# A convolution, attention and mixture kernel: another order for the first three images of its first part, and VectorE as a second engine for their norms and copies

## The chip, the cores and the metric

The kernel runs on one core of a Trainium2 chip. The metric is the device time of one execution in microseconds (us), given as the median over several executions. The engines are TensorE (PE in the profile), VectorE (DVE), ScalarE (ACT), GpSimd (POOL) and SyncE (SP, which issues the transfers). "PEld" is TensorE's weight load.

## The reference

The input is x with 32 images of 128 channels and 64x64 pixels. Layer 0 normalises each image over groups of four channels, multiplies it from both sides with complex 64x64 matrices (products of butterfly factors), mixes the channels at each of the 64x64 frequencies with weights that went through such matrices too, transforms back and adds the result to x. Layer 1 is an attention over channels and a mixture of eight experts on the 4096 tokens of each image. Only the beginning of layer 0 matters here:

```python
def _gn(v, G=32, eps=1e-5):
    g = v.reshape(B_, G, C_ // G, H_, W_)
    m = jnp.mean(g, axis=(2, 3, 4), keepdims=True)
    s = jnp.var(g, axis=(2, 3, 4), keepdims=True)
    return ((g - m) / jnp.sqrt(s + eps)).reshape(v.shape)

x_f = tensor_product(xc, _c(k11), _c(k12), False)      # both axes of every image
prod = jnp.einsum('bihw,oihw->bohw', x_f, w_f)         # channels mixed at each frequency
out = tensor_product(prod, _c(k21), _c(k22), True)
x = x + jnp.real(out)
```

## The kernel before

The kernel has three parts. The first takes the 32 images one by one through the forward transform and writes `xf` to memory. The second mixes the channels, the third transforms back and does layer 1. The change is in the first part alone.

An image goes through these stages in the first part. All of it is in fp32.

- Load: eight transfers of 256 KB (`load`, L325), issued by SP, into one of three buffers `x`.
- Norm: eight `bn_stats` (`stats`, L332) and one aggregation on VectorE; a tiny matmul that averages over the group (`means`, L345); three tiny steps on VectorE (L350 to L352); a second tiny matmul (`variances`, L355); one tiny step (L358); a power on GpSimd (`power`, L362, for images 0 to 3 also a product and a sign, L365 and L366); then x is scaled in four quarters of 128x1024 (`scaled`): on ScalarE for images 0 to 3 (L373), on VectorE for all others (L375).
- `pz`: four groups of eight 128x128 transposes (`turn_over`, L386). Each group's result in PSUM is copied to `z` in four pieces of 64x512, two for each half r (`turned`, L396, all on ScalarE).
- `pv`: eight groups of 32 small matmuls along one axis (`along_w`, L409), each of which needs the whole of `z`. Each result is copied to `v` as 128x1024 (`w_out`, L420, all on ScalarE).
- `pf`: eight groups of eight matmuls along the other axis (`along_h`, L431), each of which needs the whole of `v`. Each result is copied to `f` (`h_out`, L441: ScalarE for two of eight groups, VectorE for the others) and stored to `xf` by two transfers (`store`, L449).

TensorE needs two instructions in the profile for each fp32 matmul, but one for a transpose. PSUM gives this part four buffers of two banks, used by `pz`, `pv`, `pf` and the tiny matmuls alike.

The order of all instructions is written out before the kernel runs. `add` enters each step with an engine, an estimated length, a due time `at` (in slots of 27.5) and what it comes after; `Plan.run` then plays these lists through and gives each engine, whenever it is free, the ready step with the earliest due time. On TensorE alone the order is the one in which the steps were entered. The finished lists are executed in order by each engine: what stands behind a waiting instruction waits too.

In steady state a slot `s` holds `pz` of image s, `pv` of image s-1 and `pf` of image s-2, interleaved in four quarters. At the start the same loop is used, so slot 0 has `pz` of image 0 alone, slot 1 `pz` of image 1 and `pv` of image 0, and slot 2 the first slot with all three stages. The matrices `pw` and `ph` of these stages are made on VectorE at the very beginning by six butterfly levels (`level`, L234 to L240; then `input_matrices`, L246 to L249).

Of the kernel before, what the change touches and what calls it, by code (L numbers as in the profile page):

```python
# [103 lines left out]
def kernel(  # L104
# [15 lines left out]
    nc = tc.nc  # L120
    B = x.shape[0]
# [11 lines left out]
    pf = dram.tile([n, n, P * n], F32, name="pf")  # L133
# [42 lines left out]
    with ExitStack() as ph1:  # L176
# [12 lines left out]
        def add(key, engine, us, at, run, after=(), take=(), free=(), late=0.0):  # L189
            after = [made[k] for k in after if k in made]  # L190
            if engine == "PE":
                after += on_pe[-1:]
            made[key] = plan.add(engine, us, SLOT * at, run, after, take, free, late)
            if engine == "PE":
                on_pe.append(made[key])
# [132 lines left out]
        def stats(b, k):  # L328
# [3 lines left out]
                nc.vector.bn_stats(tile_of["bs", b][:, k, :], xs[b][:, k * 512 : (k + 1) * 512])  # L332
            return run

        def group_norm(b):

            v = {}

            def moments():
                v["mv"] = st.tile([P, 2], F32, name=f"gmv{b}", tag="gmv", bufs=2)  # L340
                nc.vector.bn_aggr(v["mv"], tile_of["bs", b].rearrange("p k s -> p (k s)"))

            def means():
                v["ps"] = pp.tile([P, 2, 512], F32, tag="ps", name=f"gps{b}")
                nc.tensor.matmul(v["ps"][:, 0, 0:1], gmean, v["mv"][:, 0:1], start=True, stop=True)  # L345

            def spread():
                ms, mv = st.tile([P, 4], F32, name=f"gms{b}", tag="gms", bufs=2), v["mv"]
                v["ms"] = ms
                nc.vector.tensor_copy(ms[:, 0:1], v["ps"][:, 0, 0:1])  # L350
                nc.vector.tensor_sub(ms[:, 1:2], mv[:, 0:1], ms[:, 0:1])
                nc.vector.scalar_tensor_tensor(ms[:, 2:3], ms[:, 1:2], ms[:, 1:2], mv[:, 1:2], ALU.mult, ALU.add)  # L352

            def variances():
                nc.tensor.matmul(v["ps"][:, 0, 1:2], gmean, v["ms"][:, 2:3], start=True, stop=True)  # L355

            def shifted():
                nc.vector.tensor_scalar_add(v["ms"][:, 3:4], v["ps"][:, 0, 1:2], GN_EPS)  # L358

            def power():  # L360
                v["rstd"] = st.tile([P, 1], F32, name=f"grstd{b}", tag="grstd", bufs=2)
                nc.gpsimd.tensor_tensor(v["rstd"], v["ms"][:, 3:4], mhalf[:, 0:1], ALU.pow)  # L362
                if b < 4:
                    v["nmr"] = st.tile([P, 1], F32, name=f"gnmr{b}", tag="gnmr", bufs=2)
                    nc.gpsimd.tensor_tensor(v["nmr"], v["ms"][:, 0:1], v["rstd"], ALU.mult)  # L365
                    nc.gpsimd.tensor_scalar_mul(v["nmr"], v["nmr"], -1.0)  # L366

            def scaled(k):
                def run():
                    part = xs[b][:, k * 1024 : (k + 1) * 1024]  # L370
                    if b < 4:

                        nc.scalar.activation(part, part, AF.Identity, bias=v["nmr"], scale=v["rstd"])  # L373
                        return
                    nc.vector.tensor_scalar(part, part, v["ms"][:, 0:1], v["rstd"], ALU.subtract, ALU.mult)  # L375
                return run

            return moments, means, spread, variances, shifted, power, [scaled(k) for k in range(4)]

        def turn_over(b, g):  # L380
# [5 lines left out]
                    nc.tensor.transpose(pv[:, k, :], xs[b][:, h * n : (h + 2) * n], ident)  # L386
            return run

        def turned(b, g, r):

            def run():
                if g == 0 and r == 0:
                    zs[b] = zp.tile([P, n, n], F32, tag="z", name=f"z{b}")
                pv = tile_of["pz", b, g].rearrange("w u (k c) -> w (u k) c", c=P)
                for half in range(2):
                    nc.scalar.copy(  # L396
                        zs[b][half * n : (half + 1) * n, :, 32 * r + 8 * g : 32 * r + 8 * g + 8],
                        pv[r * n : (r + 1) * n, :, half * n : (half + 1) * n].rearrange("w h c -> w c h"),
                    )
            return run  # L400
# [14 lines left out]
        def w_out(b, g):  # L415

            def run():
                if g == 0:
                    vs[b] = vp.tile([P, n, P], F32, tag="v", name=f"v{b}")
                nc.scalar.copy(  # L420
                    vs[b].rearrange("h w (a c) -> h w a c", a=2)[:, :, :, 8 * g : 8 * g + 8],
                    tile_of.pop(("pv", b, g)).rearrange("h a (c w) -> h w a c", w=n),
                )
            return run
# [45 lines left out]
        def piece_of_image(b, k):  # L470

            add(
                ("x", b, k), "SP", 0.45, b - 2 + 0.1 * k, load(b, k),
                [("pz", b - 3, g) for g in range(4)] + [("x", b, k - 1), ("pf", b - 4, k)],
                ("x",) if k == 0 else (), (), 4.0,
            )

        def norm(b):

            at = b - 1  # L480
            for k in range(8) if b < 4 else ():
                piece_of_image(b, k)
            for k in range(8):
                add(("bn", b, k), "DVE", 0.7, at + 0.01 * k, stats(b, k), [("x", b, k), ("nm", b - 2, 3), ("bn", b, k - 1)])

        def norm_on_pe(b, step):
            if not 0 <= b < B:
                return
            at = b - 0.9
            if step == 0:  # L490
                gn = tile_of["gn", b] = group_norm(b)
                add(("ag", b), "DVE", 0.4, at, gn[0], [("bn", b, k) for k in range(8)])
                add(("g1", b), "PE", 0.3, at, gn[1], [("ag", b)], ("ps",))
                add(("gm", b), "DVE", 0.7, at, gn[2], [("g1", b)])
            else:
                gn = tile_of.pop(("gn", b))
                add(("g2", b), "PE", 0.3, at, gn[3], [("gm", b)])
                add(("gr", b), "DVE", 0.25, at, gn[4], [("g2", b)], (), ("ps",))
                add(("gp", b), "POOL", 0.6 if b >= 4 else 1.6, at, gn[5], [("gr", b)])
                for k in range(4):  # L500
                    add(("nm", b, k), *(("DVE", 0.85) if b >= 4 else ("ACT", 1.05)), at + 0.01 * k, gn[6][k], [("gp", b)])

        def piece(kind, b, g, at):
            if not 0 <= b < B:
                return
            if kind == "pz":
                add(
                    ("pz", b, g), "PE", 1.0, at, turn_over(b, g), [("nm", b, k) for k in range(4)],
                    ("ps",), ("x",) if g == 3 else (),
                )  # L510
                for r in range(2):
                    add(
                        ("zo", b, g, r), "ACT", 1.2, at, turned(b, g, r),
                        [("pz", b, g)] + [("pv", b - 2, k) for k in range(8)] + ([("zo", b, 0, 0)] if g or r else []),
                        (), ("ps",) if r else (),
                    )
            elif kind == "pv":
                add(
                    ("pv", b, g), "PE", 1.12, at, along_w(b, g),
                    [("zo", b, k, r) for k in range(4) for r in range(2)] + ["wi"], ("ps",),  # L520
                )
                add(
                    ("vo", b, g), "ACT", 1.02, at, w_out(b, g),
                    [("pv", b, g)] + [("pf", b - 2, k) for k in range(8)] + ([("vo", b, 0)] if g else []), (), ("ps",),
                )
            else:
                add(("pf", b, g), "PE", 1.95, at, along_h(b, g), [("vo", b, k) for k in range(8)], ("ps",))
                on_act = g % 4 == 3
                add(("fo", b, g), "ACT" if on_act else "DVE", 1.02 if on_act else 1.22, at, h_out(b, g), [("pf", b, g)], ("f",), ("ps",))
                add(("fs", b, g), "SP", 0.9, at, store(b, g), [("fo", b, g)], (), ("f",), 5.0)  # L530
# [4 lines left out]
        norm(1)  # L535
        norm_on_pe(0, 0)
        norm_on_pe(0, 1)
        for s in range(B + 2):
            if s == 0:
                norm(2)  # L540
            for g in range(4):
                at = s + 0.25 * g
                if g == min(s, 3) - 1:
# [6 lines left out]
                for k in range(2):  # L550
                    piece("pf", s - 2, 2 * g + k, at + 0.12 + 0.07 * k)
                    if 4 <= s + 2 < B:
                        piece_of_image(s + 2, 2 * g + k)
            if 3 <= s + 2 < B:
                norm(s + 2)
            if s == 0:
                norm_on_pe(1, 0)
                norm_on_pe(1, 1)
            if s == 3:
                butterfly(0, "POOL", nc.gpsimd, 3.2, 4.5)  # L560
                add("sel", "POOL", 2.5, 99, select, [("nm", 4, 3)])
# [8 lines left out]
            if 12 <= s < 16:  # L570
                k = s - 12
# [11 lines left out]
    with ExitStack() as ph2:  # L583
# [162 lines left out]
        for w in range(n):  # L746
# [9 lines left out]
            for half in range(2):  # L756
                for t in range(4):
                    at = w + 0.5 * half + 0.125 * t
# [784 lines left out]
```

## Time and profile before

| | us |
|---|---|
| median of 4 runs | 5922.15 (5916.55 to 5925.2) |
| the profiled execution | 5922.91, of which 5921.1 are its span |
| TensorE busy | 5787.2 (98%) |
| VectorE busy | 4234.0 (72%) |
| ScalarE busy | 3830.1 (65%) |
| GpSimd busy | 3944.3 (67%) |
| TensorE's first transpose (image 0) | 21.12 |
| first `pv` of image 0 | 39.06 |
| first transpose of image 3 | 87.68 |
| last `pf` of the first part ends | about 928 |

The span runs from the first to the last instruction. All times within it are counted from its start. The page of the profile gives busy times and a strip of 40 slices of the span for each engine, in tenths; the timeline lists instructions in order with the idle time before them and what ended it.

### The profile page before, as it was taken

How to read it: one execution, taken by the hardware profiler on the slowest of the kernel's cores; microseconds unless marked ns; L12 is line 12 of the kernel's file. 1: busy time of each engine (PE TensorE's matmuls, PEld its weight loads, DVE VectorE, ACT ScalarE, POOL GpSimd, SP SyncE). 2: the span in 40 equal slices, each digit the busy share in tenths (PEclk: the TensorE clock that was granted, in tenths of full speed). 3: DMA queues.
4: the chain of work that ended last, by engine and by line, in shares of the span. 5: the costliest groups of instructions: out<-in, count | busy, mean ns of one | idle time of the engine just before them, and what ended most of it. 6: DMA issues, size and time to landing. Idle time of an engine off the chain costs nothing.

```text
span 5921.1 us, 221064 instructions
## 1 busy us (share of the span) xinstructions
PE 5787.2 (98%) x94348; PEld 4559.5 (77%) x94348; DVE 4234.0 (72%) x10353; ACT 3830.1 (65%) x7089; POOL 3944.3 (67%) x4210
## 2 busy tenths in 40 slices
PE   7999999999999999989999999999999999999997
PEld 7999999999999999976666666666666666666653
DVE  5565555555555555537888878788888888787877
ACT  7666664555555555457777777777777777777762
POOL 2110006666666666607888888888888888888887
PEclk9999999999999999989999999999999999999999
DMA  5766667666666666652322222222223222222201
GB/s 196 239 228 234 236 212 208 172 170 173 172 172 172 172 172 173 162 153 61 97 76 87 78 79 87 82 88 83 89 75 97 76 84 81 79 86 84 77 21 29
DMA packets 664682, 756.90 MB, mean 128 GB/s; under 512 B 70608, under 2 KB 462288, under 8 KB 659600
## 3 DMA queue, kind: packets, MB, share of 16 engines
q1 hardware_dynamic: 661088, 733.69, 42.4%
q8 instruction: 741, 12.14, 0.9%
q0 software_dynamic: 2608, 9.06, 0.5%
q14 instruction: 245, 2.01, 0.1%
HBM read 406.79 MB, written 335.54 MB: 125 GB/s over the span
## 4 chain that ended last, share of the span: by engine, by line
PE 81%; DVE 12%; ACT 3%; issue 2%; POOL 2%; DMA 1%; SPq 0%; DVEq 0%; POOLq 0%; ACTq 0%
PE pe L1323 24%; PE m L671 17%; PE g L649 10%; PE pf L431 7%; PE pu L910 4%; PE py L933 4%; PE pp L1185 4%; PE pg L1112 4%; DVE tm L1334 4%; PE pv L409 3%; DVE bs L1035 2%; PE pz L386 1%; ACT z L396 1%; PE px L1310 1%; PE pt L1066 1%
## 5 line engine op out<-in xcount | busy, mean ns | idle before, releaser
L1323 PE MATMUL pe<-ew_sb,xT 128*128 128x512 f32 x4096 | 1973.3, 600 | 36.4 <-DVE tm L1334 22.6
L1334 DVE TENSOR_TENSOR tm<-pe,oh 128x512 f32<-128x512 f32 x2028 | 1296.0, 676 | 369.7 <-PE pe L1323 261.6
L1359 POOL TENSOR_TENSOR tm<-tm 128x512 f32<-128x512 f32 x1014 | 1269.3, 1270 | 291.0 <-DVE tm L1334 287.1
L1323 PEld LDWEIGHTS pe<-ew_sb,xT 128*128 128x128 f32 x4096 | 692.0, 190 | 551.6 <-issue 325.5
L660 DVE COPY f<-g 128x1024 f32<-128x1024 f32 x508 | 622.0, 1224 | 649.7 <-PE g L649 649.6
L671 PE MATMUL m<-f,s 128*64 128x64 f32 x32768 | 1070.6, 224 | 2.4 <-issue 1.6
L671 PEld LDWEIGHTS m<-f,s 128*64 128x64 f32 x32768 | 1000.6, 138 | 63.7 <-issue 3.0
L617 POOL COPY s<-l 128x512 f32<-128x512 f32 x512 | 547.3, 1105 | 524.1 <-issue 507.9
L660 ACT COPY f<-g 128x1024 f32<-128x1024 f32 x508 | 514.4, 1013 | 561.8 <-PE g L649 535.3
L1362 POOL TENSOR_TENSOR tk<-tk,tm 128x256 f32<-128x256 f32 x1014 | 736.5, 726 | 79.5
L1360 POOL TENSOR_TENSOR tm<-tm 128x512 f32<-128x512 f32 x507 | 644.0, 1270 | 39.8
L649 PE MATMUL g<-c,wst 9*128 9x128 f32 x16256 | 599.4, 283 | 4.1 <-issue 3.9
L921 ACT COPY u<-pu 64x512 f32<-64x512 f32 x960 | 556.4, 580 | 69.2 <-PE pu L910 60.1
L1196 ACT ACTIVATE pp<-pp,ln 128x128 f32<-128x128 f32 x1024 | 440.6, 430 | 232.5 <-PE pp L1185 160.4
L649 PEld LDWEIGHTS g<-c,wst 9*128 9x128 f32 x16256 | 502.5, 186 | 38.8 <-issue 4.2
L619 POOL TENSOR_SCALAR s<-l 128x512 f32<-128x512 f32 x256 | 510.5, 1994 | 0.0
L362 POOL TENSOR_TENSOR grstd<-gms,mhalf 128x1 f32<-128x1 f32 x32 | 17.7, 552 | 735.4 <-DVE gms L358 735.4
L431 PE MATMUL pf<-ph,v 128*128 128x128 f32 x4096 | 491.2, 278 | 6.5 <-issue 1.8
L910 PEld LDWEIGHTS pu<-qw,r 128*128 128x128 f32 x3840 | 458.3, 193 | 34.2 <-ACT u L921 22.1
L431 PEld LDWEIGHTS pf<-ph,v 128*128 128x128 f32 x4096 | 466.9, 192 | 16.4 <-ACT z L396 7.1
L910 PE MATMUL pu<-qw,r 128*128 128x128 f32 x3840 | 472.7, 277 | 5.1 <-ACT u L921 5.0
L1035 DVE BATCH_NORM_STATS2 bs<-tk 128x6 f32<-128x128 f32 x2048 | 448.5, 277 | 27.6 <-ACT tk L1071 26.3
(176 smaller groups left out, 7964.8 us busy)
## 6 DMA issues: line engine op xcount, KB each, us to landing
xf<-f SPq DMA_DIRECT2D x512, 256.0 KB
pf<-o SPq DMA_DIRECT2D x1016, 128.0 KB
l<-xf SPq DMA_DIRECT2D x1012, 128.0 KB
r<-pf SPq DMA_DIRECT2D x496, 256.0 KB
x<-in_x_dram SPq DMA_DIRECT2D x256, 256.0 KB
out_dram<-so SPq DMA_DIRECT2D x1024, 64.0 KB
y<-in_x_dram SPq DMA_DIRECT2D x31, 2048.0 KB
r<-pf POOLq DMA_DIRECT2D x16, 248.0 KB, 8.4
```

The source lines that it names most:

```text
L431: nc.tensor.matmul(pl[:, j * P : (j + 1) * P], vs[b][:, 8 * g + j, :], ph.rearrange("h r m -> h (r m)"), start=True, stop=True,)
L649: nc.tensor.matmul(pg[g // 2][:, g % 2, m * P : (m + 1) * P], wst[rows, 16 * half + 4 * t + m, :], c[rows].rearrange("r h k -> r (h k)"), ...
L660: copy(f.rearrange("i m (g o) -> i m g o", g=2), tile_of["g", w, half, t][k].rearrange("i g (o m) -> i m g o", o=4))
L671: nc.tensor.matmul(ps[hh * n : (hh + 1) * n, q, :], s[:, h].rearrange("i k b -> i (k b)")[:, B * r : B * r + n], f[:, h, r, :], start=(r = ...
L910: nc.tensor.matmul(ps[:, k, :], rs[b, e][:, k * P : (k + 1) * P], qw.rearrange("w r m -> w (r m)"), start=True, stop=True,)
L921: nc.scalar.copy(u[r * n : (r + 1) * n, :, oh * n + 8 * e : oh * n + 8 * e + 8], ps[oh * n : (oh + 1) * n, :, r * n : (r + 1) * n].rearran ...
L1035: nc.vector.bn_stats(bs[:, i - lo, :], t[:, i, :])
L1323: nc.tensor.matmul(ps, tile_of["xT", b, i // 4][:, i % 4, :], ew_sb[:, es, :].rearrange("d e c -> d (e c)"), start=True, stop=True,)
L1334: nc.vector.tensor_tensor(tile_of["tm", b, i // 2][:, i % 2, es, :], tile_of.pop(("pe", b, i, half)).rearrange("p (e c) -> p e c", c=P), t ...
L1359: nc.gpsimd.tensor_tensor(tm[:, k, 0:4, :], tm[:, k, 0:4, :], tm[:, k, 4:8, :], ALU.add)
L1360: nc.gpsimd.tensor_tensor(tm[:, :, 0:2, :], tm[:, :, 0:2, :], tm[:, :, 2:4, :], ALU.add)
L1362: nc.gpsimd.tensor_tensor(t[:, lo : lo + 2, :], t[:, lo : lo + 2, :], tm[:, :, m, :], ALU.add)
```

## The change

Four things are done, all in the first part and all for images 0 to 3.

- The order of TensorE's work is written out for the first three images in place of slots 0 to 2 of the loop: `pz` of image 0, `pv` of image 0, `pf` of image 0 with `pz` of image 1 between its groups, `pv` of image 1 with `pz` of image 2 between its groups. The loop begins at slot 3, where it finds the same state as before: image 3 is to be transposed, image 2 to go through `pv`, image 1 through `pf`.
- The norms of images 2 and 3 and two quarters of image 0's are scaled on VectorE and no longer on ScalarE; for images 2 and 3 the two extra steps on GpSimd go.
- Of the copies to `z`, half r = 1 of groups 0 to 2 of image 0, of all groups of image 1 and of groups 2 and 3 of image 2 go to VectorE. Of the copies to `v`, the odd groups of image 0 go to VectorE.
- The due times of the norms of images 1 to 3 are other ones, and the loads of image 4 are entered elsewhere.

From slot 3 on, the lists of all engines are the same as before, apart from the buffers' numbers.

```diff
+        def on_dve(b, k):
+            return b >= 2 or (b == 0 and k >= 2)
...
-                if b < 4:
+                if b < 2:
                     v["nmr"] = st.tile([P, 1], F32, name=f"gnmr{b}", tag="gnmr", bufs=2)
...
-                    if b < 4:
+                    if not on_dve(b, k):
                         nc.scalar.activation(part, part, AF.Identity, bias=v["nmr"], scale=v["rstd"])
                         return
                     nc.vector.tensor_scalar(part, part, v["ms"][:, 0:1], v["rstd"], ALU.subtract, ALU.mult)
...
+        def z_on_dve(b, g, r):
+            return r == 1 and (g < 3 if b == 0 else b == 1 or (b == 2 and g >= 2))
...
+                copy = nc.vector.tensor_copy if z_on_dve(b, g, r) else nc.scalar.copy
                 for half in range(2):
-                    nc.scalar.copy(
+                    copy(
                         zs[b][half * n : (half + 1) * n, :, 32 * r + 8 * g : 32 * r + 8 * g + 8],
...
-                nc.scalar.copy(
+                copy = nc.vector.tensor_copy if b == 0 and g % 2 else nc.scalar.copy
+                copy(
                     vs[b].rearrange("h w (a c) -> h w a c", a=2)[:, :, :, 8 * g : 8 * g + 8],
...
-            at = b - 1
+            at = {1: -0.2, 2: 0.45, 3: 1.3}.get(b, b - 1)
...
-            at = b - 0.9
+            at = {1: -0.1, 2: 0.6, 3: 1.6}.get(b, b - 0.9)
...
-        for s in range(B + 2):
-            if s == 0:
-                norm(2)
+        for g in range(4):
+            piece("pz", 0, g, -0.4)
+        for g in range(8):
+            if g == 6:
+                norm_on_pe(1, 0)
+            piece("pv", 0, g, 0.02 * g)
+        norm_on_pe(1, 1)
+        norm(2)
+        for g in range(8):
+            if 3 <= g < 7:
+                piece("pz", 1, g - 3, 0.3 + 0.08 * g)
+            piece("pf", 0, g, 0.3 + 0.08 * g)
+            if g == 3:
+                norm_on_pe(2, 0)
+            if g == 5:
+                norm_on_pe(2, 1)
+        norm(3)
+        for g in range(8):
+            if g >= 4:
+                piece("pz", 2, g - 4, 1.0 + 0.08 * g)
+                piece_of_image(4, 2 * g - 8)
+                piece_of_image(4, 2 * g - 7)
+            piece("pv", 1, g, 1.0 + 0.08 * g)
+            if g == 3:
+                norm_on_pe(3, 0)
+            if g == 5:
+                norm_on_pe(3, 1)
+        norm(4)
+        for s in range(3, B + 2):
...
-            if 3 <= s + 2 < B:
+            if s + 2 < B:
                 norm(s + 2)
-            if s == 0:
-                norm_on_pe(1, 0)
-                norm_on_pe(1, 1)
```

Here `norm(b)` enters the loads and `bn_stats` of image b, `norm_on_pe(b, 0)` the aggregation and the first tiny matmul with the steps behind it, and `norm_on_pe(b, 1)` the second tiny matmul, the power and the scaling.

More of the change, by code (lines that the diff above doesn't have):

```diff
@@ L498, in norm_on_pe @@
                 add(("gr", b), "DVE", 0.25, at, gn[4], [("g2", b)], (), ("ps",))
-                add(("gp", b), "POOL", 0.6 if b >= 4 else 1.6, at, gn[5], [("gr", b)])
+                add(("gp", b), "POOL", 0.6 if b >= 2 else 1.6, at, gn[5], [("gr", b)])
                 for k in range(4):
-                    add(("nm", b, k), *(("DVE", 0.85) if b >= 4 else ("ACT", 1.05)), at + 0.01 * k, gn[6][k], [("gp", b)])
+                    add(("nm", b, k), *(("DVE", 0.85) if on_dve(b, k) else ("ACT", 1.05)), at + 0.01 * k, gn[6][k], [("gp", b)])
         def piece(kind, b, g, at):
@@ L512, in piece @@
                     add(
-                        ("zo", b, g, r), "ACT", 1.2, at, turned(b, g, r),
+                        ("zo", b, g, r), *(("DVE", 1.4) if z_on_dve(b, g, r) else ("ACT", 1.2)), at, turned(b, g, r),
                         [("pz", b, g)] + [("pv", b - 2, k) for k in range(8)] + ([("zo", b, 0, 0)] if g or r else []),
@@ L522, in piece @@
                 add(
-                    ("vo", b, g), "ACT", 1.02, at, w_out(b, g),
+                    ("vo", b, g), *(("DVE", 1.22) if b == 0 and g % 2 else ("ACT", 1.02)), at, w_out(b, g),
                     [("pv", b, g)] + [("pf", b - 2, k) for k in range(8)] + ([("vo", b, 0)] if g else []), (), ("ps",),
```

## The prediction

> **What bounds the kernel now.** I read the page first: where is TensorE not full, and where not at full clock?
>
> ```profile
> span 5921.1 us, 221064 instructions
> PE   7999999999999999989999999999999999999997
> PEclk9999999999999999989999999999999999999999
> ```
>
> A slice is 148 us. TensorE has room only in the first slice, at the hand-over to the second part (slice 18, where the clock dips too) and in the last. The change touches the first slice, so its worth is read there, not from averages. Next, TensorE's timeline of the opening (start, length, instructions, idle before and what ended it):
>
> ```profile
> 21.12 5.83 PE L386 MATMUL pz<-ident,x 128*128 128x128 f32 x32 [4.07 <-ACT x L373]
> 36.77 0.56 PE L345 MATMUL gps<-gmv,gmean 128*128 128x1 f32 x2 [4.34 <-DVE gmv L341]
> 39.06 3.67 PE L409 MATMUL pv<-pw,z 64*64 64x64 f32 x128
> 51.09 3.69 PE L409 MATMUL pv<-pw,z 64*64 64x64 f32 x128 [4.07 <-ACT z L396]
> 87.68 1.04 PE L386 MATMUL pz<-ident,x 128*128 128x128 f32 x8
> 88.65 2.10 PE L409 MATMUL pv<-pw,z 64*64 64x64 f32 x128
> 90.67 3.84 PE L431 MATMUL pf<-ph,v 128*128 128x128 f32 x32
> 94.35 1.04 PE L386 MATMUL pz<-ident,x 128*128 128x128 f32 x8
> ```
>
> At 87.68 image 3 is first transposed; from there both orders of every engine are the same. The last four rows give steady steps, start to start: a pz group 0.97 us, two pv groups 2.02 (1.01 each), two pf groups 3.68 (1.84 each). Work between 21.12 and 87.68 is 12 pz, 16 pv and 8 pf: 11.6 + 16.2 + 14.7 = 42.5 us. The stretch is 66.6 us, so 24 us are lost, to waiting or to half clock (the pairs at 39.06 and 51.09 take 3.7 us instead of 2.1). That is the most this change can touch. Who is late? ScalarE's timeline:
>
> ```profile
> 24.38 9.46 ACT L396 COPY z<-pz 64x512 f32<-64x512 f32 x16
> 33.92 4.64 ACT L373 ACTIVATE x<-x,gnmr,grstd 128x1024 f32<-128x1024 f32 x4
> 45.21 4.63 ACT L373 ACTIVATE x<-x,gnmr,grstd 128x1024 f32<-128x1024 f32 x4
> ```
>
> ScalarE runs nearly without a gap: copies of image 0, norm of image 1, norm of image 2 in the middle of image 0's pv. VectorE meanwhile idles 19.4 us up to 64.26. So ScalarE and the order set the opening.
>
> **Prices.** The groups by shape up to 960 us, then VectorE's timeline:
>
> ```profile
> L396 ACT COPY z<-pz 64x512 f32<-64x512 f32 x512 | 296.6, 579 | 157.8 <-PE pz L386 153.2
> L441 DVE COPY f<-pf 128x1024 f32<-128x1024 f32 x192 | 230.7, 1215 | 168.9 <-PE pf L431 158.2 <-DMA xf<-f 4.9 <-DMA x<-in_x_dram 4.1
> ```
>
> ```profile
> 22.50 1.17 DVE L234 TENSOR_TENSOR bp<-tw,bf 128x64 f32<-128x64 f32 x8
> 25.59 4.84 DVE L332 BATCH_NORM_STATS2 gbs<-x 128x6 f32<-128x512 f32 x8
> 105.52 2.98 DVE L375 TENSOR_SCALAR x<-x,gms,grstd 128x1024 f32<-128x1024 f32 x4 [0.75 <-POOL grstd L362]
> 108.41 2.35 DVE L441 COPY f<-pf 128x1024 f32<-128x1024 f32 x2
> ```
>
> Start to start: a norm quarter on VectorE 2.89/4 = 0.72 us (ScalarE 4.64/4 = 1.16); bn_stats 4.84/8 = 0.605; a 128x1024 copy out of PSUM 1.14 (110.68 - 108.41 over two). A 64x512 copy on VectorE is not in the trace. Ends: 0.57 (half of 1.14) and 1.14 (as long as twice the elements). I take 0.60, near the first: two copies of one size differ little between engines here (ScalarE 0.58 for 64x512, 1.01 for 128x1024), and the strided 128x1024 evictions of part two cost VectorE the same 1.22 as plain ones.
>
> **What moves.** Ten norm quarters (two of image 0, all of images 2 and 3), 9 pairs of z copies (3, 4 and 2 of images 0, 1, 2) and 4 v copies go from ScalarE to VectorE. ScalarE loses 10x1.16 + 18x0.58 + 4x1.01 = 26 us; VectorE gets 10x0.72 + 18x0.60 + 4x1.14 = 22.6 us, in a queue that holds bn_stats and f copies too. So VectorE becomes the engine to follow. GpSimd loses two tiny products for images 2 and 3 (about 0.45 us each time), worth nothing to the sum: VectorE's norms of image 2 have 0.4 us to spare when the power is ready. SP issues the same loads; image 3's still wait for image 0's last transpose (about 25 us), image 4's for image 1's (about 60 us), over 10 us before their bn_stats. I cost those at nothing; a late one would cost its own delay.
>
> **The new chain, stage by stage** (us from the span's start).
> 1. Image 0, pv starts. VectorE at 22.50: two norm quarters 1.44, last butterfly level and matrices 25.59 - 22.50 = 3.09, six z copies 3.6: 30.6. ScalarE is done earlier (its ten copies end near 28). pv 0 starts at 30.7 instead of 39.06.
> 2. pv of image 0. TensorE has stood for 5 us, so three groups run at half clock (1.8 each), five at 1.01, and two small matmuls 0.5: 41.6. VectorE is queued behind eight bn_stats of image 1 (30.6 + 4.84 + 0.3 = 35.8), then v1, v3, the small group-norm steps, v5 (41.2), a step that waits for the matmul at 41.6, and v7: 42.9. pf starts at 43.0. The queue costs 1.4 us here: the step waits, v7 stands behind it, and every pf behind v7.
> 3. pf of image 0 with pz of image 1: three pf, pz, pf = 8.3, so 51.3. The next small matmul needs image 2's aggregate, and VectorE has from 42.9 eight bn_stats, three f copies, two z copies and the aggregate, 4.8 + 3.4 + 1.2 + 0.3 = 9.7: 52.6 to 52.7. TensorE waits 1.5. Then 0.25 + 3x0.97 + 4x1.84 + 0.25 = 10.8: 63.6. VectorE meanwhile must do image 2's four norms ahead of the last two z copies of image 1 (59.2 small step, 60.3 after f5, 63.2, 64.4). pv of image 1 starts at 64.5, 0.9 late.
> 4. pv of image 1 with pz of image 2: 8x1.01 + 4x0.97 + 0.5 = 12.5, 77.0 at best, with 0.5 for image 3's aggregate and 0.6 for a PSUM buffer: 78.1 for image 3's first transpose. ScalarE holds v0 to v7 and 12 z copies and finishes image 2's last z copy only at 80.2 (from 70.3: 12x0.59 + 3x0.92), so pv of image 2 starts 1.3 behind its transpose.
> The steady order is thus reached as if at 79.4, not 87.68: 8.3 us earlier. Every later wait of TensorE up to 900 us is 1.5 us in sum or less, and what ends them moves along, so the end moves by the same. The profiled run took 5922.91 us, of them 5921.1 in the span; minus 8.3 it is 5914.6. It lies 0.76 above the median of 5922.15, so I say 5914.
>
> [...] The clock, at TensorE's idle stretch from 47.02 to 51.09 (columns: window, TensorE busy, clock, DMA):
>
> ```profile
> 48.00:49.00 1.00, 0.00 (x0) 1.00 0.00 0
> 49.00:50.00 1.00, 0.00 (x0) 0.70 0.00 0
> 50.00:51.00 1.00, 0.00 (x0) 0.50 0.00 0
> ```
>
> The clock fell near 49.5, only 2.5 us after the last matmul. By this row the 5 us before pv of image 0 do cool it, as I summed, and the 1.5 us in stage 3 do not, but would at about 2.5.
> [...]
>
> **Bounds.** A z copy at 0.57 gives 0.4 us more; each 0.1 us above 0.60 takes 1.4, as about 14 of 18 lie on the chain. If the clock never falls before pv, stage 2 gains 1.8, VectorE then being last. If it falls at one of the later gaps, as between 51.09 and 56.45 in the profile (5.4 us at half speed), that is 2.6 lost. My steps are good to 2 us over five stages. So the gain is 3.5 to 11 us, 5911 to 5918.6; the runs before spread over 8.7 us, half of which I add on each side: 5907 to 5923.
>
> **Rivals.**
> - *Clock and gaps better than I think.* TensorE keeps its clock (1.8), the waits of 1.5, 0.9 and 1.8 in stages 3 and 4 vanish: 14.3 us, 5908. For it: the clock stayed full from 27 to 32.5 in the profile with little work. Against: VectorE's queue has hardly a gap left, and the order fixes it.
> - *Slower: strided copies on VectorE.* Place: the 64x512 z copies. If they cost 1.14, the chain grows by 14x0.54 = 7.6, the waits of stage 3 pass 2.5 us and the clock falls twice (5.2): 4.5 us slower, 5926.6. It decides from 0.82 us a copy with two clock falls ((8.3 - 5.2)/14 more than 0.60), from 1.19 without. Against: the strided evictions quoted above.
> - *Given back.* The opening is shorter but the hand-over near 929 us starts when something else is ready: 5922. Against: the first loads there are released by a transpose and the first copies by a v copy of part one, so they move too.
>
> **Numbers.** Forecast 0.70, better clock 0.15, slow copies 0.07, given back 0.08. A measurement tells about 0.2% (11.8 us) from no change. Beyond that on the fast side lie most of the second case and a little of my own tail, 0.20; on the slow side only a worse form of the third, 0.05; 0.75 is within. The range 5907 to 5923 leaves out the low end of the second case and the third.
>
> **What would show it.** Image 3's first transpose near 78 us and pv of image 0 near 30.7; VectorE without a gap of over 2 us between 22 and 78; z copies on VectorE at 0.6 to 0.7 us; half clock once, after 31 us; and the same distance between image 3's first transpose and the end of the span, less 1.3 us, as before. I am wrong if TensorE waits for VectorE by more than 2.5 us at image 2's aggregate, or if that distance changes by more than 4 us.

## The result, and the profile after

The changed kernel takes 5926.24 us (median of 41 runs, 5918.26 to 5934.63), the kernel before 5920.57 beside it (61 runs, 5913.02 to 5927.7). The ratio is 1.0011 with a 95% interval of 1.0007 to 1.0015. (A ratio is estimated from the fast runs alone and need not be the quotient of the two medians.) It is slower by about 5.7 us, or 0.11%, where the forecast was 5914, 8 us faster, with a range of 5907 to 5923.

TensorE's strip on the page, and two of the page's rows (instructions of each engine; packets, MB and share of the DMA queue that carries instructions):

```profile
span 5922.9 us, 221055 instructions
PE   7999999999999999979999999999999999999997
PE 5784.8 (98%) x94348; PEld 4556.4 (77%) x94348; DVE 4257.0 (72%) x10385; ACT 3805.1 (64%) x7057; POOL 3943.0 (67%) x4206
q8 instruction: 740, 12.12, 0.9%
```

The strip doesn't show what happened: the first slice is a 7 as before. TensorE's timeline of the opening does (start, length, instructions, idle before and what ended it):

```profile
31.30 0.48 PE L414 MATMUL pv<-pw,z 64*64 64x64 f32 x4 [3.25 <-DVE z L401]
32.02 5.17 PE L414 MATMUL pv<-pw,z 64*64 64x64 f32 x180 [0.25 <-DVE z L401]
38.42 2.10 PE L414 MATMUL pv<-pw,z 64*64 64x64 f32 x128 [1.22 <-issue]
41.87 1.28 PE L414 MATMUL pv<-pw,z 64*64 64x64 f32 x72 [1.36 <-issue]
43.39 1.04 PE L414 MATMUL pv<-pw,z 64*64 64x64 f32 x54
45.33 1.37 PE L414 MATMUL pv<-pw,z 64*64 64x64 f32 x74 [0.90 <-issue]
48.48 5.59 PE L437 MATMUL pf<-ph,v 128*128 128x128 f32 x48 [1.47 <-DVE v L426]
58.51 0.35 PE L348 MATMUL gps<-gmv,gmean 128*128 128x1 f32 x2 [1.77 <-DVE gmv L344]
70.84 0.33 PE L414 MATMUL pv<-pw,z 64*64 64x64 f32 x4 [1.03 <-DVE z L401]
78.38 3.41 PE L414 MATMUL pv<-pw,z 64*64 64x64 f32 x116 [4.52 <-issue]
92.03 1.09 PE L388 MATMUL pz<-ident,x 128*128 128x128 f32 x8
```

Image 0's `pv` starts 7.8 us earlier than in before, and image 3's first transpose comes 4.35 us later. Four idle times inside `pv`, 8.0 us in sum, are marked "issue": no semaphore, buffer or engine that the profile knows ended them. A record is one matmul entry of the profile. The first three idle times come after 184, 312 and 438 of image 0's `pv` records (440 with the two of a small matmul at 43.08, left out above): 128 apart, which are 256 instructions with the loads, and inside groups of 64, where no matmul waits for a copy. In before the same stretch has 0.3 us of them.

What TensorE lacks there are its own instructions. The page counts 94348 + 94348 matmul and load instructions and 740 packets on queue q8, 12.12 MB: 255 instructions and 16 KB a packet. A `pv` group is 64 records of each kind, so two of them back to back (1.01 us a group) use a packet in 2.02 us. The trace has the packets of image 0's `pv` at 36.06, 39.56, 42.99 and 46.43 us: 3.45 us apart, each 0.93 to 0.96 us long, with hardly any other traffic. These 3.45 us have two parts: TensorE starts again 2.3 us after a packet begins (at 38.42, 41.87 and 45.33), and the next packet begins 1.1 us after that. A steady quarter (`pz`, two `pv`, two `pf`) holds 336 instructions in 6.67 us, a packet in 5.1 us; there the supply suffices (1.9 us of issue waits in before from 115 to 671 us).

The long stall has one thing more. Between 52.96 and 76.10 no such packet was transferred. Up to 70.84 hardly any was needed: the eight `pf` and four `pz` before it are some 330 instructions. The DMA queues in 36 to 48 us, and then in 65 to 77 us (packets, MB, share of the 16 engines):

```profile
q1 hardware_dynamic: 57, 0.10, 2.1%
q8 instruction: 4, 0.07, 2.0%
```

```profile
q1 hardware_dynamic: 2003, 3.66, 95.2%
q8 instruction: 1, 0.02, 0.5%
```

In 65 to 77 us the stores of image 0 and the loads of image 4 fill the engines, and the one instruction packet of these 12 us comes at their end. TensorE, stopped since 73.86, starts again 2.3 us after the packet, and near half clock (0.59, then 0.50 from 79 to 81 us; length, TensorE busy, clock, DMA share, GB/s):

```profile
77.00:78.00 1.00, 0.00 (x0) 1.00 1.05 393
78.00:79.00 1.00, 0.62 (x24) 0.59 0.33 125
```

### The profile page after: what moved, and what is told of

It is laid out like the page before. It is cut to its first block, busy times and chain, and to the rows that moved or that the text cites. A ratio compares the mean times of both kernels' runs of the same rounds, so it can differ in the third digit from the quotient of the medians.

```text
span 5922.9 us, 221055 instructions
## 1 busy us (share of the span) xinstructions
PE 5784.8 (98%) x94348; PEld 4556.4 (77%) x94348; DVE 4257.0 (72%) x10385; ACT 3805.1 (64%) x7057; POOL 3943.0 (67%) x4206
## 3 DMA queue, kind: packets, MB, share of 16 engines
q8 instruction: 740, 12.12, 0.9%
## 4 chain that ended last, share of the span: by engine, by line
PE 82%; DVE 12%; ACT 3%; issue 2%; POOL 1%; DMA 0%; SPq 0%; DVEq 0%; POOLq 0%; ACTq 0%
PE pe L1352 24%; PE m L700 17%; PE g L678 10%; PE pf L437 7%; PE pu L939 4%; PE py L962 4%; PE pp L1214 4%; PE pg L1141 4%; DVE tm L1363 4%; PE pv L414 3%; DVE bs L1064 2%; PE pz L388 1%; ACT z L401 1%; PE px L1339 1%; PE pt L1095 1%
```

## The experiments

Theory 1: `pv` run back to back outruns the supply of TensorE's instructions, and the new order makes two such runs. Theory 2: the copies out of PSUM, or the queues of ScalarE and VectorE, pace `pv`, and "issue" only means a wait that isn't seen. Marks are image 3's first transpose (87.68 in before, 92.03 in after). Medians are compared with runs of before on the same chip in the same session, with 11 runs a kernel unless said; they tell differences of about 5 us and more; the opening of a profile tells smaller ones, since it repeated within 1.3 us (see below).

**Fewer instructions for the same streaming.** `pv` of images 0 and 1 in after with half the matmuls, each of 128 instead of 64 columns.

```diff
+    if b < 2:
+        for k in range(0, 8, 2):
...
+            ps[r * n : (r + 1) * n, half, k * n : (k + 2) * n],
+            zs[b][rows, 8 * g + k, :], pw[rows].rearrange("p r m -> p (r m)"),
```

> The changed kernel, but pv of images 0 and 1 uses half as many matmuls of twice the columns (the same streaming time on TensorE, half the instructions; what these two images get is not the transform). Theory 1 (TensorE runs out of instructions in the long runs of pv: the stalls of 1.22, 1.36, 0.90 and 4.52 us marked issue in the profile of the changed kernel): the three short stalls go, the long one shrinks or goes, image 3's first transpose comes near 84 to 87 us instead of 92.0, and the time is 5 to 9 us below the changed kernel. Theory 2 (VectorE's strided copies and its queue set the opening; the issue label is only how the profile names it): pv ends no earlier, image 3's first transpose stays at 91 to 93, the time is within 2 us of the changed kernel.

```profile
73.22 1.10 PE L415 MATMUL pv<-pw,z 64*64 64x128 f32 x31 [1.00 <-issue]
80.89 1.09 PE L388 MATMUL pz<-ident,x 128*128 128x128 f32 x8
```

The mark came at 80.89, 11.1 us earlier than in after; of the issue waits one of 1.00 us was left. The median was 5921.98 against 5922.97 of before (ratio 0.9997, 0.9989 to 1.0006), which by the two ratios is about 8 us under after. Order, copies and their engines are those of after, so Theory 2 falls. Halving takes out weight loads too, but the stops in after came every 128 records and ended 2.3 us after a packet began, which speaks for the packets.

**Each image by itself.** The same, with `b == 0` and with `b == 1`.

> The kernel after, with pv of image 0 alone made of half as many matmuls of twice the columns (the same streaming time, half the instructions; both halves of a pair then use one stationary tile, so the values of image 0 differ). Theory 1 (TensorE waits for its own instructions where pv runs back to back): the three waits marked issue in stage 2 (1.22 + 1.36 + 0.90 = 3.5 us) go and the stall in stage 4 stays, so pf of image 0 starts at about 45 instead of 48.48 and image 3's first transpose at 87 to 90 instead of 92.03; the whole time 2 to 5 us under that of the kernel after. Theory 2 (the copies out of PSUM on ScalarE and VectorE pace pv): nothing moves, image 3's first transpose at 91 to 93.

> The same halving in pv of image 1 alone. Theory 1: stage 2 keeps its 3.5 us of waits, and the 4.52 us stall of stage 4 goes with the slower clock behind it: stage 4 (pv of image 1 and pz of image 2) takes 14 to 16 us instead of 20.4, and image 3's first transpose comes at 85 to 88. This and the run with image 0 should add up to the 11.1 us that halving both took off. Theory 2: 91 to 93.

Image 0: `pf` starts at 42.86 instead of 48.48, the stall in `pv` of image 1 stays (4.39), the mark is 86.34, a little better than forecast; the median is 5926.66 against 5925.31 (1.0005, 0.9996 to 1.0014). Image 1: the long stall shrinks to 1.25, but the mark is 90.82, not 85 to 88; 5927.11 against 5925.31 (1.0000, 0.9991 to 1.0009). So the two do not add up to 11.1. Two things stood in the way in the second: image 3's aggregate was now waited for (0.92), and the clock fell twice, after image 0's waits and, by the length of the 31 matmuls there (1.98 us, 1.10 with both images halved), after the 1.25. This is its `pf` after image 0's `pv`, beside 5.59 us for the same 48 matmuls in after, and the granted clock from 48.3 to 52 us (0.50):

```profile
48.36 8.34 PE L448 MATMUL pf<-ph,v 128*128 128x128 f32 x48 [1.47 <-DVE v L437]
```

```profile
48.30:52.00 3.70, 3.64 (x17) 0.50 0.00 0
```

**The loads of image 4 later.** In after, they come behind the last `pv` of image 1 (` + [("pv", 1, 7)]` in what they wait for).

> The changed kernel, with the eight loads of image 4 issued only after pv of image 1 (2 MB less to move between 65 and 78 us). Theory 1, second half (the 4.52 us stall at 78 is one instruction fetch that stands behind image 4's loads and image 0's stores in the DMA engines): the stall shrinks to 1 to 2 us, image 3's first transpose comes 3 to 5 us earlier, and so does the end, unless image 4's statistics come late. Rival (the stall has its length from the run of pv alone): stays at 4 to 5 us, time within 2 us of the changed kernel.

```profile
76.42 3.43 PE L414 MATMUL pv<-pw,z 64*64 64x64 f32 x116 [2.08 <-issue]
```

The stall fell from 4.52 to 2.08, so in this profile about half of it went with the loads. But another wait of 1.45 appeared 10 us later, and the mark was 92.42: nothing gained (5929.68 against 5922.97, 1.0010, 1.0001 to 1.0019).

**The two halves of the change.** The sharing with VectorE alone, in before's order; and the new order alone, with all these norms and copies on ScalarE.

> The kernel before with its own order of TensorE's work, and only the sharing of norms and copies with VectorE. Theory 1: the old order mixes transposes between pairs of pv, so instructions keep up; ScalarE was the late engine there; 4 to 9 us below the kernel before. Theory 2 (VectorE's copies are what costs): within 2 us of the kernel before or slower.

> The changed order of TensorE's work, with all norms of images 0 to 3 and all z and v copies on ScalarE as before. Theory 1: the stalls of pv stay and ScalarE is late as well, 3 to 12 us above the changed kernel. Theory 2: VectorE's queue is gone from the chain, so it is no slower than the changed kernel, or faster.

The sharing alone came to 5927.5 against 5922.97 (1.0008, 0.9999 to 1.0017), mark 89.81, where I had expected a gain; the order alone to 5931.07 (1.0014, 1.0006 to 1.0023), by the two ratios about 2 us above after and not 3 to 12. Their telling rows, first the sharing, then the order:

```profile
33.94 0.56 PE L348 MATMUL gps<-gmv,gmean 128*128 128x1 f32 x2 [6.59 <-DVE gmv L344]
42.61 0.56 PE L348 MATMUL gps<-gmv,gmean 128*128 128x1 f32 x2 [6.28 <-DVE gmv L344]
```

```profile
69.35 1.03 PE L414 MATMUL pv<-pw,z 64*64 64x64 f32 x53 [0.74 <-issue]
88.86 1.97 PE L388 MATMUL pz<-ident,x 128*128 128x128 f32 x8 [5.46 <-ACT x L375]
```

In before the two small matmuls of images 1 and 2 came at 30.99 and 36.77. With image 0's norm quarters and z copies in VectorE's queue, the statistics behind them are 3 and 6 us late. So neither half of the change pays alone.

The order alone did not do what Theory 1 forecast of it: the stalls of `pv` did not stay. They were 0.34, 0.79 and 0.74, against 8.0 us in after, and what made this version late is the norm of image 3 on ScalarE (5.46). Image 0's `pv` ran at half clock until about 39 us there (an estimate from its 312 records in 7.93 us beside 2.02 for 128), and at half clock two groups took 3.67 us in before (at 39.06, clock 0.50), longer than the 3.45 between packets. That doesn't explain the 0.74: the DMA engines were 93 to 99% busy from 64 to 70 us, as in after, yet the packet came at 66.83, 0.5 us after image 1's `pv` had started. In after it came 5.3 us after that start. Full DMA engines alone therefore don't make the long stall.

**Many rows of four `pv`.** Before, its opening untouched; in slots 4 to 23 each half slot is `pz`, `pf`, `pz`, `pf`, four `pv`, two `pf`. Then the same order with the halved instructions in images 3 to 22.

```diff
-    piece("pz", s, g, at)
-    for k in range(2):
-        piece("pv", s - 1, 2 * g + k, at + 0.04 + 0.04 * k)
...
+    elif g % 2 == 0:
+        for k in range(2):
+            piece("pz", s, g + k, at + 0.1 * k)
+            piece("pf", s - 2, 2 * g + k, at + 0.1 * k + 0.04)
+        for k in range(4):
+            piece("pv", s - 1, 2 * g + k, at + 0.2 + 0.04 * k)
```

> The kernel before, its opening untouched, with the pv of slots 4 to 23 brought together: each half slot is pz, pf, pz, pf, then four pv in a row, then pf, pf, instead of pairs of pv between pz and pf. The work is the same. Theory 1: four pv are 512 instructions in 4.04 us, two packets more than lie ready, at 3.45 us a packet; so each row of four should wait 1.4 to 2.5 us for instructions, twice a slot in 20 slots: 40 to 80 us slower than the kernel before, with waits marked issue inside pv. Theory 2 (a bunch of copies on ScalarE): slower too, but with waits on ScalarE's copies, and as much slower in the run with halved instructions.

> The same order as the run with four pv in a row, with the instructions of pv halved in images 3 to 22 (values of these images differ; streaming time, copies and order are the same). Theory 1: within 10 us of the kernel before, no waits marked issue in these slots. Theory 2: as slow as the run with four pv in a row, within 10 us.

Four in a row: 6098.33 (2 runs) against 5925.31, ratio 1.0293 (1.0274 to 1.0312): 173 us for an order of the same work. All that TensorE waited for in these slots, by the waits (us in total, times, longest), and its clock in 300 to 500 us (0.88; in before 1.00):

```profile
PE pv L409 <- issue: 108.0, 37, 5.4
PE pf L431 <- issue: 19.1, 12, 4.0
```

```profile
300.00:500.00 200.00, 166.54 (x3715) 0.88 0.55 176
```

With half the instructions, in the same order: 5902.18 (3 runs), 0.9961 (0.9946 to 0.9976), no wait marked issue in these slots. So the order harms only through the number of instructions. My sizes were off both ways. Waits were 3.2 us a row (127.1 over 40 rows) where I had put 1.4 to 2.5, and 173 - 127 = 46 us are left; the lower clock, which I had left out, is the likely taker, by this difference alone. Of the waits over 0.5 us, 44 in number, each ended 2.2 to 4.1 us after a packet began (median 2.4). The halved kernel is 23 us faster than before and not level with it: a halved group takes 0.92 us (3.66 for four, start to start) instead of 1.01, which is 15 us over 20 slots; the remaining 8 I have not traced.

**Two versions that keep `pv` apart.** Before with the norms of images 2 and 3 on VectorE and nothing else (`b < 4` becomes `b < 2`); and after with `pv` of image 1 mixed with the last `pf` of image 0 and `pz` of image 2.

> The kernel before with one part of the change alone: the norms of images 2 and 3 go to VectorE (4 x about 0.8 us each) instead of ScalarE; order, z copies and v copies stay. In before, TensorE waits 4.07 us at 51.09 for z copies of image 1 that queue on ScalarE behind four norms of image 2. Theory 1 (each pair of pv stays between pz and pf, so instructions arrive in time; sharing all copies in the earlier run failed because VectorE's own z copies and norms of image 0 stood in front of the statistics of images 1 and 2): that wait goes, the statistics stay on time (image 1's aggregate at about 31), and image 3's first transpose comes at 81 to 84 instead of 87.68. The whole time is then 2 to 7 us under before. Rival (any sharing delays the statistics on VectorE): the aggregates come later and image 3's first transpose at 87 or later.

> The kernel after, with the order of stages 3 and 4 changed so that pv of image 1 does not run back to back: the last pf of image 0 and the transposes of image 2 are put between its groups. Theory 1: the wait of 4.52 us in stage 4 shrinks to under 2, the waits of stage 2 (3.5 us, pv of image 0) stay; image 3's first transpose at 82 to 87 instead of 92.03. Rival (TensorE's instructions do not matter there, image 4's loads and the norm of image 3 do): 90 or later.

```profile
47.81 1.84 PE L409 MATMUL pv<-pw,z 64*64 64x64 f32 x106 [0.48 <-issue]
83.13 1.04 PE L386 MATMUL pz<-ident,x 128*128 128x128 f32 x8
```

Norms alone: 5922.67 against 5927.27, ratio 0.9991 (0.9983 to 1.0000), mark 83.13, as forecast. The wait of 4.07 us at 51.09 is gone; in its place are four waits for instructions of 0.5 to 1.0 us, 2.5 in sum, where `pv` pairs now follow each other faster. This is the best version of the study with all of before's work in it, though its interval reaches no change; against after, by the two ratios, it is 0.2% faster. The mixed one: 5928.11 (1.0003, 0.9994 to 1.0013), mark 89.29, less than expected. Its long stall became 0.99 and 0.79, but image 0's `pv` still ran back to back (4.3 us of waits), and the `pf` behind it took 5.56 us for 32 matmuls, 1.7 more than the 3.84 of the steady ones; by these lengths the clock was low there.

**How far one profile goes.** Both kernels once more.

> The kernel before once more, for its profile: how far one profile stands for the kernel. If the opening is set by waits that repeat, image 3's first transpose falls within 1.5 us of 87.68, and what the profile differs in comes after it, in waits marked issue of under 1 us each and in part 2: the distance from there to the end (5823.3 us in the first profile) may differ by 4 us.

> The kernel after once more, for its profile. If the waits for instructions repeat: 3 to 4 us marked issue in stage 2, 3.5 to 5 us in one piece in stage 4, image 3's first transpose within 1.5 us of 92.03. If they were an accident of the first profile, they are gone or elsewhere. Distance from there to the end (5820.8 us in the first profile) within 4 us.

Before: mark 88.35. After: 93.31, with issue waits of 2.23, 0.71 and again one long one:

```profile
79.60 3.47 PE L414 MATMUL pv<-pw,z 64*64 64x64 f32 x116 [4.63 <-issue]
```

So the opening repeats within 1.3 us, the waits with it. From the mark to the end it doesn't: 5823.3 and 5829.9 us in before, 5820.8 and 5834.9 in after, counted to the end of TensorE's last matmul, which lies 10.1 us before the end of the span in all four. Two profiles of one kernel differ by more than 4 us, as I had not expected.

## Why the prediction was wrong

By its own stages, in us:

| | predicted | after | after again |
|---|---|---|---|
| 1: `pv` of image 0 starts | 30.7 | 31.30 | 30.39 |
| 2: from there to `pf` of image 0 | 12.3 | 17.18 | 18.30 |
| 3: to `pv` of image 1 | 21.5 | 22.36 | 23.25 |
| 4: to image 3's first transpose | 13.6 | 21.19 | 21.37 |
| the sum | 78.1 | 92.03 | 93.31 |

**The step that failed** is the price of a `pv` group in stages 2 and 4, "five at 1.01" and "8x1.01". It was read from steady pairs, which stand between `pz` and `pf`, and carried to eight groups in a row. Back to back, 256 instructions were used up in 2.02 us and the next 256 came after 3.45. Stage 2 is 4.9 too long: 3.5 are waits for instructions, and 0.7 pass between the start of the first four matmuls and the next, while the last z pieces are copied; 0.7 I can't place. Stage 4 is 7.6 too long: 4.52 the stall, 1.6 the slower clock behind it (3.41 for 116 records, 1.83 at full clock), 0.6 more waits for z copies than summed; 0.9 I can't place. The halved instructions took 10.4 us off these two stages (12.29 and 15.66 us; the other 0.7 of the 11.1 lie before them), of which about 1.5 is the shorter halved group, 16 times 0.09. Rows of four elsewhere brought the loss back: this cause is shown. Not shown is what sets the 3.45 us between packets, nor the whole of the long stall. Of its 4.52, 3.45 - 2.02 = 1.4 would be the same lack as in image 0's `pv`, by an estimate from these two figures. The rest goes with the packet that came only at 76.10. Issuing the loads later took 2.4 off, but the order alone, with the DMA engines as full, stood only 0.74.

**What held.** Stage 1, VectorE's queue in stage 2 (the wait for v7: 1.4 forecast, 1.47 found), the aggregate of image 2 (1.5 forecast, 1.77 found, under the 2.5 I had set) and half clock after the pause before `pv` (0.50 from 31.3 to 36 us, behind a pause of 3.25 us; 5 were forecast). It came a second time, behind the long stall (0.50 from 79 to 81 us). **A term of the wrong size** was the z copy on VectorE:

```profile
27.61 4.26 DVE L401 COPY z<-pz 64x512 f32<-64x512 f32 x6
```

0.71 us each, not 0.60, within its bounds; by the prediction's own 1.4 us for each 0.1 it is worth 1.5 us.

**"The end moves by the same"** can't be judged by the distance I named, from the mark to the end of the span, since it differs by 6.6 and 14.1 us between two profiles of one kernel. By medians it holds for the change: about +5.7, beside +5.1 and +6.35 for image 4's first transpose against the mean of before's two profiles (115.35). It holds for the norms alone (-4.6 beside -4.9). It holds less well for the halved instructions of both images, -1.0 (-6.5 to +3.6) beside -6.0, and for the order alone, +8.1 beside +3.35. Beside the first profile of before, that of the halved instructions gives 2.9 us back between images 16 and 30, in steps of 0.4 to 0.7 at small issue waits; beside the second it is 1.1, so this isn't settled.

**The rivals.** None came: no step waited on slow strided copies enough to decide (0.71 lies under 0.82), and nothing was given back at the hand-over (the first matmul behind it, at 929.23 in before and 936.08 in after, is 1.19 us late in both). The case that came was not among them, though its first sign was in before's trace: an issue wait of 0.29 at 62.61, in the `pf` that follows a quicker stretch of `pv`.

What the supply cost went with the order: 1.9 us of issue waits in the steady slots of before (115 to 671 us), with 255 instructions a packet as in after, and 127 us in 20 slots with rows of four `pv`.

## What to carry to other kernels

Before work is put together on an engine, count its instructions against time: the small matmuls here, 1.01 us a group between longer work, used up 256 instructions in 2.02 us when put together, and a packet of them came every 3.45 us. Mixed with work that has few (336 instructions in 6.67 us) they lost 1.9 us to issue waits in 556 us. Look also at which transfers land where such a row runs: issuing 2 MB later took 2.4 us off a stall here, though nothing off the time. Before a queue is shared out, look what stands behind each moved piece: moving eight norm quarters gave about 4.6 us (an interval that reaches no change), and moving the copies and image 0's norm as well lost it.

## What was not expected of the hardware

- Instruction packets of 16 KB came 3.45 us apart though each took 0.93 to 0.96 us and the DMA engines were all but idle (4.1% busy from 36 to 48 us); with the engines 95% full from 65 to 77 us one came, at 76.10, and TensorE stood for 4.52. Engines as full let one through within 0.5 us of the start of `pv` in the run of the order alone.
- Short gaps came before a low clock, as one gap of 4.07 us did in before (0.50 from 50 to 55 us): with image 1 halved, gaps of 0.68, 1.91, 1.17 and 1.47 within 12 us were followed by a clock of 0.50 for 3.7 us. Nearly the same gaps in after (1.22, 1.36, 0.90 and 1.47) were not followed by it (clock 1.00 from 48.5 to 54 us). The prediction had let gaps of 1.5 us pass as harmless.
